# Broadcasting a score row to all partitions in two DMA loads of 512 columns instead of one of 1024 (a four-layer graph attention kernel)

## The chip, the cores and the metric

The kernel runs on one core of a Trainium2 chip. The metric is the device time of one execution in microseconds (us); lower is better. Engines are called PE (TensorE, matmuls), PEld (its weight loads), DVE (VectorE), ACT (ScalarE), POOL (GpSimd) and SP (SyncE, which here only issues DMAs).

## The reference: what is computed

16 graphs of 1024 nodes with 256 features, a 0/1 adjacency of 1024 x 1024 for each, and four attention layers in a row, each added to its input:

```python
h = jnp.maximum(_layernorm(x, axis=-1), 0.0)
x = x + _L0_gnn_ref(h, adj, ...)      # 4 heads of 64; the same for layers 1, 2; layer 3 has one head of 256
# inside a layer, for each head:
e = leaky_relu(s1[:, None] + s2[None, :], slope)     # s1, s2: one number a node, h @ (W a)
attention = softmax(where(adj == 0, -inf, e), axis=-1)
out = attention @ (h @ W)
```

Layer 2 adds a bias, a relu, the projected h and a layernorm over each head before its result is added.

## The kernel before

All the work is in `fast_path` (line 537). A *unit* is one layer of one graph. The 48 units with four heads (layers 0 to 2) run in the fixed order `ORDER` (lines 412 to 419), which mixes graphs so that one unit's preparation lies beside another's attention; the 16 units of layer 3 are fitted in between.

A unit is prepared in `prepare` (line 949): statistics, normalisation (`normal`), transposes and projection to `v` (`project`). For each head there is then one row of 1024 numbers, an exponential of the nodes' scores. The exponential of a sum under a leaky relu is a maximum of two products, so an attention tile needs only this row spread over all partitions, one number a partition (`fac`) and the mask.

The row gets to all partitions through DRAM. It is written to a scratch `line` (lines 1119 to 1121) and read back with an access pattern whose first dimension has step 0, so that each of 128 partitions receives the same 4 KB (lines 1123 to 1130):

```python
over = units.tile([P, N], F32, name="rows", bufs=ROWS)      # ROWS = 1; rows_one for layer 3
sp.dma_start(over, bass.AP(tensor=flat.tensor, offset=flat.offset + h * N, ap=[[0, P], [1, N]]))
```

There is one buffer `rows`, so the next head's load waits until ACT has copied the last row away. `spread_row` (line 1209) lets ACT copy the row to a two-bank PSUM tile `r`; `cover` (line 1218) lets DVE make eight tiles `p` of 128 x 1024 from it, each `max(r, fac) * mask`; `gather` (line 1278) lets PE multiply the tile's 64-column pieces with `v`, 65 columns at a time, into `po`; `evacuate` and `finish` take the sums away. For layer 3 `last_layer` (line 1396) reads `rows_one` in pieces.

The order of instructions on every engine is written by a planner at build time. `Plan` (line 443) holds for each engine when it would be free and adds an assumed cost for each instruction (`cost`, line 463; a DMA costs 400 ns of the SP queue). The loop at line 1589 takes, among all steps that could go next, the earliest one. A step is a piece of a Python generator up to its next `yield`, which names the engine of the next piece. Nothing is reordered later: each engine, SP's queue among them, runs its list in order and waits where a semaphore says so. The SP queue also carries the loads of `x_cur`, the transposing loads of the masks (`mask<-near`), weights, and the stores to `out`; the adjacency is cast on its way to the scratch `near` by DMAs of the POOL queue.

Of the kernel before, what the change touches and what calls it, by code (L numbers as in the profile page):

```python
# [20 lines left out]
P = 128  # L21
# [400 lines left out]
SPREAD = 0  # L422
SOONER = 300.0
AT_ONCE = -(10**6)
ACT_STATS = (0,)
SETTLE = 83.0
SECOND = 4000.0
# [109 lines left out]
def fast_path(  # L537
# [21 lines left out]
    nc = tc.nc  # L559
    ctx.enter_context(tc.manual_schedule())  # L560
    plan = Plan()
    pe, act, dve, pool, sp = (
        plan.engine(e, name)
        for e, name in (
            (nc.tensor, "PE"),
            (nc.scalar, "ACT"),
            (nc.vector, "DVE"),
            (nc.gpsimd, "POOL"),
            (nc.sync, "SP"),
        )  # L570
    )
    G, N, F = x.shape
# [82 lines left out]
    def bank():  # L655
        k = min(free_banks(), key=lambda k: banks[k])
        banks[k] = None
        if k >= BANKS:
            spare[0] += 1
            return ps_o.tile([P, 512], F32, name="po"), k  # L660
        return ps_p.tile([P, 512], F32, name=f"pp{k}"), k

    def drop(k: int):
        banks[k] = plan.now
# [17 lines left out]
    def wide_bank(dt=F32):  # L682
        k = wide_free.index(min(t for t in wide_free if t is not None))
        wide_free[k] = None
        return ps_r.tile([P, 4096 // mybir.dt.size(dt)], dt, name=f"r{k}"), k

    def leave_wide(k: int):
        wide_free[k] = plan.now
# [3 lines left out]
    def weights(layer: int):  # L692
# [43 lines left out]
        for k in range(KC):  # L736
            for c in range(KC):
                to = c * KC + k
                pe.transpose(pw[:, to * P : (to + 1) * P], given[:, k, c * P : (c + 1) * P], ident)
        yield "ACT", None, AT_ONCE  # L740
        if n == 1:
# [4 lines left out]
        drop(at)  # L746
        yield "PE", free_bank, AT_ONCE + 1
        pa, at = bank()
        for k in range(KC):
            for half in range(0, P, P // 2):  # L750
                for c in range(KC):
# [6 lines left out]
                    )  # L758
        yield "ACT", None, AT_ONCE
        act.copy(wa[layer][:, :, :, w : w + 2], pa[:, : KC * 2 * n].rearrange("p (k h c) -> p k h c", k=KC, h=n))  # L760
# [116 lines left out]
    def normal(es: list, rs: bass.AP):  # L877
# [25 lines left out]
        for e in es:  # L903
            yield "ACT", None, AT_ONCE
            e.hT = work.tile([P, KC, 2 * P], F32, name="hT", bufs=PAIRS)
# [5 lines left out]
    def project(e, i: int):  # L911
# [16 lines left out]
        e.read = plan.now  # L928
        yield "ACT", None, AT_ONCE
        act.copy(u.v[:, 2 * e.pair + i, :width], pv[:, :width])  # L930
# [18 lines left out]
    def prepare(u: "Unit"):  # L949
# [3 lines left out]
        width = n * (w + 2)  # L953
        by_act = layer in ACT_STATS and u.g.b >= BY_ACT and (layer < 3 or u.g.b < G - 2)
        yield "ACT" if by_act else "DVE", lambda: (
# [14 lines left out]
        if by_act:  # L970
            for i in range(2 * NB):
# [6 lines left out]
                b, c = i % NB, i // NB  # L978
# [48 lines left out]
        turned(pm, mine[:, 1, :])  # L1027
        yield "DVE", None, AT_ONCE
        top = small.tile([P, 1], F32, name="top", bufs=3)
# [16 lines left out]
        c = small.tile([P, 4, MAXN], F32, name="c", bufs=2)  # L1046
# [35 lines left out]
        if direct:  # L1082
# [20 lines left out]
            else:  # L1103
                yield "DVE", None, AT_ONCE
                over = units.tile([P, N], F32, name="rows_one", bufs=1)
# [16 lines left out]
        flat = line[: n * NB]  # L1122
        for h in range(len(u.row), n):
            yield "SP", lambda: (u.before is None or len(u.before.ps) == u.before.many * NB) if n == 1 else taken(ROWS, 4 * u.turn + h)
            if n > 1:
                over = units.tile([P, N], F32, name="rows", bufs=ROWS)
            else:
                over = units.tile([P, N], F32, name="rows_one", bufs=1)
            sp.dma_start(over, bass.AP(tensor=flat.tensor, offset=flat.offset + h * N, ap=[[0, P], [1, N]]))
            u.row.append((over, plan.now))  # L1130
        if n == 1:
            add(u.until + LATE, last_layer(u), plan.now)

    def turned(to, of):

        for half in range(0, P, P // 2):
            pe.matmul(to[half : half + P // 2, : P // 2], of, ident[:, half : half + P // 2])

    def taken(count: int, k: int):

        k -= count
        return k < 0 or main[k // H].weighed > k % H
# [59 lines left out]
    def row_due():  # L1202

        if rowed[0] == len(main) * H or rowed[0] * NB - at_tile[0] > ROW_LEAD or not free_wide():
            return False
        u, h = main[rowed[0] // H], rowed[0] % H
        return len(u.row) > h and max(u.row[h][1], free_wide())

    def spread_row():

        u, h = main[rowed[0] // H], rowed[0] % H
        rowed[0] += 1
        r, k = wide_bank()
        act.copy(r, u.row[h][0])
        u.across[h] = r, k, plan.now
        u.weighed += 1
# [179 lines left out]
    def last_layer(u: "Unit"):  # L1396

        due = lambda: (
            u.ready
            and hasattr(u, "flat")  # L1400
            and at_tile[0] >= u.gate
            and not row_due()
            and (late[0] < LATE_TILES or (at_tile[0] == len(tiles) and room() is not None and late[0] < TILES - 1))
        )
        free = lambda: due() and free_wide() and max(u.g.loaded, u.ready, free_wide())
        soon = lambda: u.ready and at_tile[0] == len(tiles) and room() and late[0] < TILES - 1 and max(u.ready, room())
        begun = at_tile[0]
        part = N // u.many
        for i in range(u.many):
            if i == 1:  # L1410
                add(u.until + LATE_SUMS, last_sums(u), plan.now)
            for j in range(0, NB, u.many):
                if u.kept:
                    yield "DVE", soon
                    late[0] += 1
                    cover_late(u, i, j, u.kept[0][:, i * part : (i + 1) * part])
                    continue
                yield "ACT", free, begun + LATE + int((i * NB + j) * SPREAD)
                late[0] += 1
                r, at = wide_bank()  # L1420
                act.copy(r[:, :part], u.row[0][0][:, i * part : (i + 1) * part])
                yield "DVE", room, at_tile[0]
                cover_late(u, i, j, r[:, :part])
                leave_wide(at)
        if u.kept:
            leave_wide(u.kept[1])
# [157 lines left out]
    def add(until, gen, ready, first=None):  # L1584
        jobs.append([until, ready, *(first or next(gen))[:2], gen])
# [3 lines left out]
    while True:  # L1589
        while begins and (begins[0][0] <= at_tile[0] or not jobs):  # L1590
            _, gen, until = begins.pop(0)
            add(until, gen, 0.0)
        can = []

        def offer(engine, ready, until, what):
            can.append((max(plan.free[engine], ready), until, engine, what))

        if row_due():
            offer("ACT", row_due(), at_tile[0], "row")
        if at_tile[0] < len(tiles) and room() is not None:  # L1600
            u, h, j = tiles[at_tile[0]]
            if h in u.across and u.g.loaded and u.ready:
                offer("DVE", max(u.across[h][-1], u.g.at[j % NQ2], u.ready, room()), at_tile[0] + SLACK, "cover")
        first = reach()
        if first:
            offer("PE", first[0], at_tile[0] + SLACK, "gather")
        for job in jobs:
            ready = job[3] is None or job[3]()
            if ready:
                ready = max(job[1], ready)  # L1610
                engine = job[2]
                offer(engine, ready, job[0], job)
        if not can:
            assert not jobs and not begins and at_tile[0] == len(tiles), "nothing can go on"
            break
        best = {}
        for e in ("SP", "POOL", "DVE", "ACT", "PE"):
            mine = [c for c in can if c[2] == e]
            if mine:
                first = min(c[0] for c in mine)  # L1620
                best[e] = min((c for c in mine if c[0] <= first + NEAR), key=lambda c: c[1])
        when, _, engine, what = min(best.values(), key=lambda c: c[0])
        plan.now, plan.last = when, None
        if what == "row":
            spread_row()
        elif what == "cover":
            cover(*tiles[at_tile[0]])
            at_tile[0] += 1
        elif what == "gather":
            gather()  # L1630
        else:
            step = next(what[4], None)
            if step is None:
                jobs.remove(what)
            else:
                wait = 0.0 if step[0] == engine else MARGIN.get(step[0], 40.0) if at_tile[0] < len(tiles) else 40.0
                what[0] = step[2] if len(step) > 2 else what[0]
                what[1:4] = [(when if step[0] == engine else plan.now) + wait, *step[:2]]


    nc.vector.tensor_scalar(bad[:, 2:3], greatest[:, G * LAYERS - 1 :], 1.0 / LEAST, bad[:, 3:4], ALU.is_le, ALU.is_lt)  # L1641
# [47 lines left out]
```

## Time and profile before

| | |
|---|---|
| time, median of 3 runs | 2668.85 us (2665.5 to 2671.96) |
| time of the profiled execution | 2667.53 us |
| its span, first to last instruction | 2665.8 us |
| granted TensorE clock, mean | 0.997 |
| loads of a row (`rows`, `rows_one`) | 190 + 13, 512 KB each |
| ACT copies of a row to PSUM | 190, 1021 ns each |
| DMA queue q1 (hardware) | 143088 packets, 159.10 MB |
| DMA queue q0 (POOL's, the `near` loads) | 67456 packets, 16.78 MB |
| HBM traffic | 191.77 MB read, 34.39 MB written |

Busy time is the union of an engine's instructions. In the waits view a row says who waited for whom, then the total in us, how often, and the longest. "issue" as the one waited for means that no semaphore explains the wait. In the timeline a row has the start, the length, the engine, the line, the operation, how many were merged (xN), and in brackets the idle time before it. Nearly all instructions carry line L515, the helper that records them, so they are told apart by tiles.

### The profile page before, as it was taken

Reading aid. Unit: us, or ns where it says so; the run is one execution under the profiler, and the core shown is the slowest. Engines: PE = TensorE matmul, PEld = TensorE weight load, DVE = VectorE, ACT = ScalarE, POOL = GpSimd, SP = SyncE. Lnnn points to the kernel's source line nnn. Section 1 sums busy time; section 2 is a strip of 40 time slices with the busy share of each in tenths; the row PEclk is TensorE's granted clock in tenths of the full one; section 3 lists DMA queues with packets and bytes.
Section 4 is the critical chain, followed back from the end, with each engine's and each line's share of the span. In section 5 each row is a group of like instructions: output and inputs, shape, how many; then the busy total and the mean of one; then the engine's idle time right before and its main releaser. Section 6 shows DMA issues by size and latency. Waiting matters only on the chain. (4 is left out here: it accounts for less than half of the span.)

```text
span 2665.8 us, 132436 instructions
## 1 busy us (share of the span) xinstructions
PE 2578.2 (97%) x59354; PEld 2207.9 (83%) x59354; DVE 2342.0 (88%) x3723; ACT 1272.3 (48%) x3378; POOL 1890.4 (71%) x3375
## 2 busy tenths in 40 slices
PE   9999999999999999999999999999999999899998
PEld 7888887787988788889888788988778798888775
DVE  6799998897999797889998897999888699998984
ACT  4633563654346456533564644356364553443441
POOL 5556888765778877747887875688787565977761
PEclk9999999999999999999999999999999999999999
DMA  8533233443132253313314441323334441111100
GB/s 133 84 75 73 59 69 69 76 87 71 64 66 63 63 85 82 76 57 77 72 55 82 88 72 59 83 50 75 74 74 79 83 85 57 53 47 55 40 23 32
DMA packets 211122, 184.44 MB, mean 69 GB/s; under 512 B 150640, under 2 KB 184560, under 8 KB 210544
## 3 DMA queue, kind: packets, MB, share of 16 engines
q1 hardware_dynamic: 143088, 159.10, 20.7%
q0 software_dynamic: 67456, 16.78, 10.3%
q8 instruction: 467, 7.65, 1.2%
q14 instruction: 111, 0.91, 0.1%
HBM read 191.77 MB, written 34.39 MB: 85 GB/s over the span
## 5 line engine op out<-in xcount | busy, mean ns | idle before, releaser
L515 DVE SCALAR_TENSOR_TENSOR p<-r,fac,mask 128x1024 f32<-128x1024 f32 (+2 forms) x2032 | 2075.7, 1079 | 159.8 <-PE pp L515 80.8
L515 PE MATMUL po<-v,p 128*64 128x65 f32 x32992 | 1060.9, 224 | 36.4 <-issue 15.8
L515 PEld LDWEIGHTS po<-v,p 128*64 128x64 f32 x32992 | 1021.5, 138 | 87.9 <-issue 30.8
L515 PEld LDWEIGHTS po<-v_flat,p 128*64 128x64 f32 x16384 | 507.8, 138 | 56.8 <-issue 24.4
L515 PE MATMUL po<-v_flat,p 128*64 128x65 f32 x16384 | 525.0, 223 | 29.4 <-issue 14.7
L515 PE MATMUL pp<-wa,hT 128*64 128x264 f32 (+1 forms) x4032 | 474.2, 385 | 0.1
L515 PE MATMUL pp<-v_one,p 128*64 128x257 f32 x3584 | 403.6, 380 | 3.2 <-ACT y L515 2.9
L515 PEld LDWEIGHTS pp<-wa,hT 128*64 128x64 f32 x4032 | 278.4, 137 | 132.1 <-ACT v L515 0.4
L515 PEld LDWEIGHTS pp<-v_one,p 128*64 128x64 f32 x3584 | 248.6, 136 | 128.0 <-ACT y L515 4.6
L515 POOL TENSOR_SCALAR hn<-x_cur,rs 128x256 f32<-128x256 f32 x504 | 274.6, 558 | 33.3 <-PE pp L515 29.3
L515 POOL TENSOR_TENSOR att<-att,inv 128x512 f32<-128x512 f32 x128 | 133.7, 1045 | 221.2 <-DVE inv L515 207.7
L515 ACT COPY att<-po 128x260 f32<-128x260 f32 x256 | 96.2, 376 | 377.1 <-PE po L515 353.1
L515 ACT COPY v<-pp 128x264 f32<-128x264 f32 (+1 forms) x392 | 148.5, 379 | 215.0 <-PE pp L515 213.8
L515 POOL TENSOR_TENSOR x_cur<-att,x_cur 128x512 f32<-128x512 f32 x190 | 225.8, 1188 | 14.9
L515 ACT COPY r<-rows 128x1024 f32<-128x1024 f32 x190 | 194.0, 1021 | 21.8 <-DVE p L515 15.5
L515 ACT ACTIVATE att<-att,s 128x64 f32<-128x64 f32 x512 | 190.9, 439 | 23.3 <-POOL s L515 23.0
L515 ACT ACTIVATE hT<-pp 128x512 f32<-128x512 f32 x250 | 136.4, 598 | 128.1 <-PE pp L515 127.4
L515 ACT ACTIVATE att<-po,inv 128x64 f32<-128x64 f32 x512 | 118.7, 321 | 145.6 <-DVE inv L515 143.6
L515 POOL TENSOR_TENSOR y<-y,x_cur 128x256 f32<-128x256 f32 x116 | 84.3, 732 | 131.6 <-ACT y L515 112.1
L515 POOL TENSOR_TENSOR v<-v,fac 128x512 f32<-128x512 f32 x131 | 136.2, 1064 | 11.5 <-ACT fac L515 11.4
L515 DVE BATCH_NORM_STATS2 st<-x_cur 128x6 f32<-128x256 f32 x400 | 138.3, 411 | 3.3 <-DMA x_cur<-in_x_dram 2.9
L515 PE MATMUL pp<-ident,hn 128*128 128x128 f32 x1000 | 137.0, 280 | 0.2 <-DVE row L515 0.2
(124 smaller groups left out, 2150.0 us busy)
## 6 DMA issues: line engine op xcount, KB each, us to landing
rows<-line SPq DMA_DIRECT2D x190, 512.0 KB
out_dram<-y SPq DMA_DIRECT2D x128, 128.0 KB
x_cur<-in_x_dram SPq DMA_DIRECT2D x112, 128.0 KB
near<-in_adj_dram POOLq DMA_DIRECT2D x112, 128.0 KB, 4.3
rows_one<-line SPq DMA_DIRECT2D x13, 512.0 KB
x_cur<-in_x_dram SPq DMA_DIRECT2D x4, 512.0 KB
line<-row SPq DMA_DIRECT2D x96, 8.0 KB
block<-in_adj_dram POOLq DMA_DIRECT2D x4, 256.0 KB, 10.4
```

Source lines behind the costliest of these rows:

```text
L515: r = call(*a, **k)
```

## The change

Each row is loaded by two DMAs of 512 columns (2 KB a partition) instead of one of 1024. The first is issued where the whole load was. The second is put on a list and issued behind the next step that the planner gives to SP; or when the planned time has gone 2.5 us further; or, at the latest, before ACT's copy that reads the row. The planner still books one load of 1024 columns. The diff, complete:

```diff
 AT_ONCE = -(10**6)
+PIECES = 2
+ROW_APART = 2500.0
 ACT_STATS = (0,)
...
                 over = units.tile([P, N], F32, name="rows_one", bufs=1)
-            sp.dma_start(over, bass.AP(tensor=flat.tensor, offset=flat.offset + h * N, ap=[[0, P], [1, N]]))
+            of = lambda c, size: bass.AP(
+                tensor=flat.tensor, offset=flat.offset + h * N + c, ap=[[0, P], [1, size]]
+            )
+            plan.spend("SP", *plan.cost("SP", "dma_start", (over, of(0, N)), {}), [flat.tensor.name])
+            size = N // PIECES
+            nc.sync.dma_start(over[:, :size], of(0, size))
+            for c in range(size, N, size):
+                pieces.append((plan.free["SP"], over[:, c : c + size], of(c, size)))
             u.row.append((over, plan.now))
...
+    pieces = []
+
+    def next_piece():
+
+        nc.sync.dma_start(*pieces.pop(0)[1:])
+
+    def all_pieces():
+
+        while pieces:
+            next_piece()
...
         r, k = wide_bank()
+        all_pieces()
         act.copy(r, u.row[h][0])
...
                 r, at = wide_bank()
+                all_pieces()
                 act.copy(r[:, :part], u.row[0][0][:, i * part : (i + 1) * part])
...
         plan.now, plan.last = when, None
+        while pieces and pieces[0][0] + ROW_APART < when:
+            next_piece()
+        waiting = len(pieces)
         if what == "row":
...
                 what[1:4] = [(when if step[0] == engine else plan.now) + wait, *step[:2]]
+        if engine == "SP" and waiting:
+            next_piece()
```

## The prediction

> **What bounds the kernel now.** First the page's busy times, then who waits for whom (all engines).
>
> ```profile
> PE 2578.2 (97%) x59354; PEld 2207.9 (83%) x59354; DVE 2342.0 (88%) x3723; ACT 1272.3 (48%) x3378; POOL 1890.4 (71%) x3375
> ```
> ```profile
> DVE p L515 <- PE pp L515: 80.8, 45, 4.9
> ...
> DVE p L515 <- PE po L515: 34.7, 30, 4.1
> DVE p L515 <- ACT r L515: 32.7, 8, 10.4
> ...
> PE po L515 <- issue: 30.5, 32, 2.6
> ...
> PE po L515 <- ACT att L515: 15.8, 16, 1.4
> ...
> PE po L515 <- DVE p L515: 9.4, 9, 2.7
> ```
>
> PE is the bound: it works 2578.2 of 2665.8 us, DVE waits for PE (80.8 + 34.7 us) far longer than PE for DVE (9.4 us). The largest item in PE's idle time is "issue", 30.5 us, a wait that no semaphore explains.
>
> What that wait is, the DMA queues tell. From the page, then from a window of 2.9 us and the 1.0 us after it:
>
> ```profile
> q1 hardware_dynamic: 143088, 159.10, 20.7%
> ...
> q8 instruction: 467, 7.65, 1.2%
> ```
> ```profile
> q1 hardware_dynamic: 132, 0.50, 51.5%
> ```
> ```profile
> q8 instruction: 1, 0.02, 5.5%
> q1 hardware_dynamic: 12, 0.02, 5.3%
> ```
>
> The timeline of PE and of SP around that window (2032.6 to 2036.5 us):
>
> ```profile
> 2027.65 9.15 PE L515 MATMUL po<-v,p 128*64 128x65 f32 x308
> 2037.83 3.95 PE L515 MATMUL po<-v,p 128*64 128x65 f32 x128 [1.02 <-issue]
> 2042.95 2.26 PE L515 MATMUL po<-v,p 128*64 128x65 f32 x71 [1.16 <-issue]
> ```
> ```profile
> 2032.64 5.29 SPq L515 DMA_DIRECT2D rows<-line  x2
> ```
>
> 467 packets of 16384 B, against 2 x 59354 PE instructions: one packet is 256 instructions, 128 matmuls with their weight loads. PE eats that in 3.95 us (the x128 row). So q8 brings PE its program, and "issue" is PE out of program. Here a row load is issued at 2032.64; q1 moves nearly all its 0.50 MB before q8's packet starts (at 2035.54, by the packet records); PE runs dry at 2036.81 and resumes 2.3 us after that start. The second row load (2037.93) does the same.
>
> It is not one case. I counted in the packet records when the 467 fetches start after the issue of the latest of the 203 row loads. By chance a half microsecond would hold about 18. There are 23 in the first half, then 9, 8, 4, 1 (0.5 to 2.5 us), then 19, 38, 27, 28, 24. Some 45 fetches are held back to behind the row. Sorting PE's stalls over 0.1 us by what moved in the 2.5 us before the late fetch: rows alone 17 stalls, 14.5 us; rows with `near` loads 4, 6.1 us; `near` alone 10, 8.4 us; the rest 8, 3.7 us.
>
> **The change part by part.** In the changed kernel the lists of PE, DVE, ACT and POOL are the same instruction for instruction; only SP's differs, by 203 more DMAs. And the words of the change mislead: 175 of the 203 second loads stand directly behind their first one, since the planner's next step is rarely SP's. 11 have an `x_cur` load between, 8 a store, 8 the other kind of row, 1 a mask transpose. So the halves are issued some 0.4 us apart.
>
> *SP's queue.* 203 issues of 0.327 us (the row loads' median) are 66 us more. SP spends 708 us waiting for ACT's copies alone, so they lie in idle time; an `x_cur` load or a store comes 0.4 us later. The list shows SP also waiting for the eighth DMA before to land; with two DMAs a row, eight reach less far back. Nearest rows: a row lands 3.8 us after issue, a store 1.9, `x_cur` 4.6. Bounds: 0, and 3 us where a burst meets it; I take 0.
>
> *Packets.* 25,984 packets of 4096 B (median 159 ns) become 51,968 of 2048 B, which the trace does not show. 1024 B packets take 46 ns, so a line gives 84: a row occupies a DMA engine 16 x 84 = 1344 ns, not 8 x 159 = 1272. Bounds: 16 x 46 = 736 and 16 x 159 = 2544 ns. I take 84, between two near rows: +0.07 us for a held fetch, 21 stalls x 0.07 = 1.5 us if nothing else changes.
>
> *The row lands later.* 0.4 us from the issue, some 0.1 from packets. ACT's copy starts 5.8 us (median) after its row has landed; 6 of 190 have under 0.4 us. ACT is idle half the time, and DVE's first tile of a row starts at least 2.2 us after the landing in all but one. That one is issued at 64.78 us: 1.73 us, and its second half goes behind a mask transpose that holds SP for 1.4 to 2.1 us. Cost between 0 and 1.5 us; I take 0.5. ACT's copy waits for two semaphores instead of one: between 0 and ACT's own idle time, taken as 0.
>
> *What a held fetch saves.* A load spends about 1.5 us on an engine (first packets 0.97 us after issue, most engines done at 2.46). If a fetch that arrives in the first half is let in between the halves, it waits up to 0.75 us less. Summing the smaller of stall and 0.75 us: 9.4 us over the 17 stalls by rows alone, and 2.9 over the 4 with `near`, of which I count half: 10.9 us. Does the engine switch there? The nearest rows are four pairs of `rows_one` and `rows` issued 0.5 to 0.8 us apart. In none did a fetch start within 3.6 us of the first issue; two started at 3.65 and 3.88, amid the second load, two at 4.86, when both were through. That speaks for a gap at the border of two DMAs (first load done at about 2.9, plus the 0.5 to 0.7 us that single rows show between their end and the fetch), not proof. Bounds: 0, and all 20.6 us of both groups. I take 10.9, since the long stalls, which make most of it, are those of fetches that came early.
>
> [...]
>
> **Sum.** 10.9 us less stall. PE also waits for ACT, DVE and POOL, some 40 us in all, so a part of what it gains is waited away: I take nine tenths, 9.8. Less 1 us for late rows and longer packets: 8.8. The profiled execution took 2667.53 us (its span 2665.8), 1.3 under the median of the runs; it would take 2658.7, the median about 2660.
>
> **Rivals.**
> - *The fetch still waits for both halves* (the change does not do what it says). For it: the halves stand back to back, and with two loads queued fetches at 4.86 us came last. Against: the two at 3.65 and 3.88. Then 0 to 3 us lost: 2669 to 2672.
> - *The split holds fetches longer.* Both halves go before the fetch and packets of 2048 B cost more than the line says. At 110 ns a row takes 16 x 110 = 1760, +0.49 us: 21 stalls x 0.49 = 10 us, and some 25 fetches now held without a stall begin to stall, at half of that, 6 us: about 2685. It decides from roughly 95 ns on. For it: in the pairs, packets of the first load took 290 to 440 ns once the second was queued. Against: 1024 B packets at 46 ns.
> - *The rows come too late.* If second halves landed 2 us later, 8 row changes where DVE already waits for ACT's copy (32.7 us) would not grow, as their rows landed over 2.4 us before; some 20 ACT copies would wait about 1 us: 5 to 10 us at most on ACT, half of it idle. 2669 to 2674. Against: only one second half lies behind a slow instruction.
>
> **Chances.** The fetch let in, 2650 to 2666: 0.58, of which 0.52 is faster by over 0.2% (5.3 us, about what a measurement of this kernel can tell from no change) and 0.06 within it. Fetch waits for both, or late rows at small price: 0.24, of it 0.04 faster by chance, 0.18 the same, 0.02 slower. Longer holds or late rows in earnest: 0.18, all slower. Together 0.56, 0.24, 0.18 + 0.02 = 0.20. The range leaves out the best of the first case (all 20.6 us gone) and the upper half of the last: 2649 to 2680. The likeliest case's own range is 2650 to 2666.
>
> **What would show it.** Right: PE's "issue" falls from 30.5 us to some 18 to 22; the stalls of about 1 us behind row loads go, those behind `near` stay; PE's busy time is unchanged; fetches start about 2.5 us after a row's first issue; 2048 B packets near 84 ns. Wrong: "issue" the same or higher, or a new row in which ACT's copy waits for `rows`. If "issue" falls and the time does not, PE's gain was waited away on DVE or ACT.

## The result, and the profile after

| | kernel before | kernel after |
|---|---|---|
| median of 20 runs each | 2667.16 us (2662.0 to 2671.96) | 2673.32 us (2665.38 to 2682.1) |
| ratio, 95% interval | 1 | 1.0024 [1.0016, 1.0032] |
| profiled execution, its span | 2667.53, 2665.8 us | 2665.38, 2663.5 us |

The change makes the kernel slower, by 0.24% or 6.2 us, where 0.3% faster was forecast. The profiled execution of after is the fastest of its 20 runs, 7.9 us under their median, so its totals must not be read as if they were the usual run's. That may be more than luck: of the kernels with a second DMA below, the change again was profiled in the second fastest of its 12 runs (7.4 us under their median), the adjacent halves in the fastest of 7 (9.9 us) and the small load in the fastest of 9 (5.3 us). Why is not known; their profiles show too little of the loss. What profiles show well is what does not vary: counts, sizes and order. First the page, busy times and queues:

```profile
PE 2581.0 (97%) x59354; PEld 2213.6 (83%) x59354; DVE 2342.1 (88%) x3723; ACT 1270.8 (48%) x3378; POOL 1885.4 (71%) x3375
...
q1 hardware_dynamic: 172320, 159.11, 21.6%
...
q8 instruction: 467, 7.65, 1.2%
```

The engines have the work they had (PE 2581.0 against 2578.2 us) and the program comes in the same 467 packets. q1 moves the same megabytes in 172320 packets instead of 143088, and its share of the DMA engines rises from 20.7 to 21.6%. Now who waits for whom, all engines:

```profile
DVE p L517 <- PE pp L517: 80.2, 45, 4.9
...
DVE p L517 <- PE po L517: 34.9, 30, 4.1
DVE p L517 <- ACT r L517: 33.0, 9, 10.4
...
PE po L517 <- issue: 27.4, 35, 2.3
...
PE po L517 <- ACT att L517: 14.8, 16, 1.4
...
PE po L517 <- DVE p L517: 12.3, 10, 2.7
...
ACT r L517 <- DMA rows<-line: 4.7, 2, 3.0
```

Each row stands where it stood before, within 3.1 us; the last one, ACT waiting for a row to land, was 3.1 us. "issue" fell from 30.5 to 27.4, not to the 18 to 22 of the forecast. Two more profiles of the same kernel, shown below, have 36.5 and 36.1 us (spans 2676.5 and 2675.4), and two more of the kernel before 35.2 and 31.5 us (2674.9 and 2670.4). One profile of each would have told the wrong sign.

The rows' DMA issues (duration of an issue, shortest/median/longest, and when the first and the last starts):

```profile
L1136 SPq DMA_DIRECT2D rows<-line x190: 319/322/396, 33.7 to 2539.5; - x190
L1147 SPq DMA_DIRECT2D rows<-line x190: 326/433/1962, 34.6 to 2539.9; - x190
```

The second halves follow 0.37 us (median) behind the first. The 51,968 packets of 2048 B take 84 ns (median), as estimated. The later half lands 4.4 us (median) after the first issue, where the whole row landed at 3.8.

What decides is when q8's packets start, counted from a row's first issue, in half microseconds from 0 to 5 us (the packet records, 467 fetches in each kernel; row loads some microsecond apart or less count as one):

```
before            23  9  8  4  1 19 36 29 26 26
before, second    20 13  8  3  1 15 37 33 25 29
before, third     19 19  4  1  1 13 49 19 29 33
after             18 16  3  3  5 20 20 32 32 23
after, second     25 11  6  3  3 14 19 40 30 25
after, third      27 12  7  4  4 16 21 33 33 23
```

In all three profiles of before the held fetches come out in a peak at 3.0 to 3.5 us (36, 37, 49); in all three of after that bin holds 19 to 21 and the peak is at 3.5 to 4.0 (32, 40, 33), in two of the three with as many in the next half microsecond.

The stretch in which the forecast wanted them, 2.0 to 3.0 us, has 25, 17 and 20 fetches against 20, 16 and 14. They are not the same kind of fetch. In the three profiles of after, 17, 16 and 17 fetches are followed, from the moment they end, by 8 or more packets of 2048 B, the last of which starts 0.9 to 1.15 us later. Eight packets are one DMA engine's share of a half (256 packets, 16 engines, two halves): these fetches were let in between the halves. One of them starts at 484.48 us, 2.98 us after the row's first issue, and takes 0.96 us; exactly 8 packets of the row start after it, from 485.43 to 486.45. The three profiles of before have no such fetch. The fetches that start 2.0 to 5.0 us after a row's first issue with 7 or fewer of its packets still to come fall from 134, 136 and 140 to 107, 104 and 103. So of the some 45 fetches that the row loads hold back, about a third is let in between the halves, and the others wait for both.

In PE's stalls over 0.1 us the two sides cancel near the row. Those of fetches that start 2.0 to 5.0 us after a row's first issue make 19.2, 24.3 and 24.8 us in the profiles of before and 17.4, 23.8 and 21.3 in those of after; all others make 12.1, 11.2 and 7.5 us before and 11.2, 13.9 and 16.0 after.

### The profile page after: what moved, and what is told of

Read it like the earlier page. It is cut to its first block, busy times and chain, and to the rows that moved or that the text cites. A ratio compares the mean times of both kernels' runs of the same rounds, so it can differ in the third digit from the quotient of the medians.

```text
span 2663.5 us, 132762 instructions
## 1 busy us (share of the span) xinstructions
PE 2581.0 (97%) x59354; PEld 2213.6 (83%) x59354; DVE 2342.1 (88%) x3723; ACT 1270.8 (48%) x3378; POOL 1885.4 (71%) x3375
## 3 DMA queue, kind: packets, MB, share of 16 engines
q1 hardware_dynamic: 172320, 159.11, 21.6%
## 5 line engine op out<-in xcount | busy, mean ns | idle before, releaser
L517 ACT COPY r<-rows 128x1024 f32<-128x1024 f32 x190 | 194.1, 1021 | 23.8 <-DVE p L517 14.7
```

Of the source, the lines that this page charges most:

```text
L517: r = call(*a, **k)
```

## The experiments

The expectations name three theories. The *program theory*: the time moves with PE's waits for its program, and fetches are let in between loads. The *window theory*: a row occupies the DMA engines for longer, from its first packet to its last, and so holds back more fetches. The *queue theory*: more DMAs make rows, stores and `x_cur` late. The one that the runs left was put in words only after the small load behind a whole row: **most of the some 45 fetches that the row loads hold wait for a second DMA directly behind a row's first as well, which moves the peak of their releases from 3.0 to 3.5 us to 3.5 to 4.0, and PE, which then waits longer for its program ("issue" 41.1 us with the small load against 31.5 before, on one chip), pays.** Rivals: the packets of 2048 B are what costs; the rows' second halves come too late; or a second DMA has a fixed price that has nothing to do with holding fetches. Each ratio is against runs of the kernel before on the same chip.

### The change again

The kernel after, unchanged.

> The changed kernel once more, for a second profile. The program theory (the time moves with PE's waits for its program, which the loads hold back; the first profile, 2665.4 us, was the fastest of 20 runs): time about 2673, and if this profile's execution is slower than the first by x us, PE's stalls (gaps with no semaphore behind them, 29.8 us in the first profile) are larger by about x. The queue theory (203 more DMAs make rows, stores and x_cur late): same time, but the additional us stand under waits of ACT for rows, DVE for r, or POOL and ACT for y, by 5 us or more in total, and PE's stalls stay near 30 us.

2685.67 us against 2676.28, 1.0035 [1.0019, 1.0052]. The loss is there on another chip, and its profile is one of the three above. Its span is 13.0 us longer than the first profile's, "issue" 9.1 us longer (36.5 against 27.4), and ACT's wait for rows no longer (4.4 us against 4.7): the time moves with PE's program, as the program theory had it, and not with late rows.

### How much the row loads hold PE back

```diff
+ONLY = 16
...
-            sp.dma_start(over, bass.AP(..., ap=[[0, P], [1, N]]))
...
+            nc.sync.dma_start(over[:, :ONLY], bass.AP(..., ap=[[0, P], [1, ONLY]]))
...
-        act.copy(r, u.row[h][0])
+        act.copy(r.rearrange("p (k c) -> p k c", c=ONLY), u.row[h][0][:, :ONLY].unsqueeze(1).to_broadcast([P, N // ONLY, ONLY]))
```

> Before, but each row load brings only 16 of the 1024 columns (64 B a partition) and ACT spreads these 16 over its 1024 columns: leaves out 63/64 of each row's load, so that the attention weights are others; every engine's list is the same. Program theory: the 14.5 us of stalls behind rows and most of the 6.1 us behind rows and near go, PE's stalls fall to 12 to 16 us, time 2645 to 2655. Queue theory and late rows: nothing waits for a row in before (3.1 us in all), so 2663 to 2668.

2646.38 us, 0.9891 [0.9871, 0.9911]. From its page and its waits:

```profile
q1 hardware_dynamic: 143088, 54.33, 9.5%
```
```profile
DVE p L516 <- PE pp L516: 79.4, 44, 4.9
...
PE po L516 <- issue: 12.1, 19, 1.3
```

The number of DMAs and packets is before's, their bytes are a third, DVE's wait for PE stays, and "issue" goes from 30.5 us to 12.1. Held fetches now start 2.0 to 3.0 us after a row's issue (54 of 467), and only two of the 20 stalls over 0.1 us that remain belong to such a fetch (0.73 and 1.24 us). So the premise of the forecast holds: row loads hold PE's program back, and what their bytes cost in all is about 30 us (2676.28 - 2646.38), more than the 20.6 us that the sorting of stalls gave as the most to be had.

### Packet size alone

One DMA a row, with its halves put 516 columns apart, so that it moves in 256 packets of 2048 B.

```diff
+WIDE = 516
...
-                over = units.tile([P, N], F32, name="rows", bufs=ROWS)
+                over = units.tile([P, 2, WIDE], F32, name="rows", bufs=ROWS)
...
+            of = bass.AP(tensor=flat.tensor, offset=flat.offset + h * N, ap=[[0, P], [N // 2, 2], [1, N // 2]])
+            sp.dma_start(over[:, :, : N // 2], of)
```

> Before, with one load a row as there, but the row in two halves 516 columns apart in SBUF, so that the one DMA has 256 packets of 2048 B. If the packets' size costs the time (twice as many packets beside near loads and fetches), about 2673 as in the changed kernel. If the number of DMAs costs it, 2667 plus or minus 1.5. The program theory has no firm view: a fetch still waits for the whole load, 1.34 instead of 1.27 us an engine, 2667 to 2669.

2677.88 us, 1.0002 [0.9989, 1.0015].

```profile
q1 hardware_dynamic: 169072, 159.10, 21.4%
```

The packets are there (143088 + 25984 = 169072), the loss is not: the second DMA costs, not the smaller packets. Its releases peak at 3.0 to 3.5 us (44 fetches), as before's do.

### The halves far apart

The second load begins one column earlier, so that it overlaps the first and has to wait until that has landed.

```diff
-                pieces.append((plan.free["SP"], over[:, c : c + size], of(c, size)))
+                pieces.append((plan.free["SP"], over[:, c - 1 : c + size], of(c - 1, size + 1)))
```

> The changed kernel, but the second load starts one column earlier and so waits for the landing of the first: the halves are about 3.3 us apart instead of 0.4. Program theory with fetches let in between: no fetch waits for more than one half (0.75 us), stalls behind rows fall from some 14 to under 5 us, time 2655 to 2662. Queue theory: SP's queue stands still for 2.9 us more at each row and rows land 3 us later, so ACT waits for rows in a quarter of the cases: 2680 or more.

2703.72 us, 1.0105 [1.0086, 1.0124]. SP's timeline and the waits:

```profile
1179.34 0.34 SPq L1136 DMA_DIRECT2D rows<-line  x1
1182.85 0.34 SPq L1147 DMA_DIRECT2D rows<-line  x1
```
```profile
ACT r L517 <- DMA rows<-line: 82.1, 30, 10.9
...
DVE p L517 <- ACT r L517: 48.7, 17, 10.6
...
PE po L517 <- issue: 24.9, 36, 1.7
```

With 3.3 us (median) between the halves, the fetches do come in between: stalls behind rows alone are 5.7 us in 9 (14.5 us in 17 before). But SP stands still for that long, a row lands 6.9 us (median) after its first issue, and ACT waits 82.1 us for rows where it waited 4 to 6 in the changed kernel. The program theory had under 5 us of such stalls and 2655 to 2662 us: it was near on the stalls and wrong on the time. What the gap gives is lost several times over in the rows.

### Always directly behind

```diff
-                pieces.append((plan.free["SP"], over[:, c : c + size], of(c, size)))
+                nc.sync.dma_start(over[:, c : c + size], of(c, size))
```

> The changed kernel, but every second load stands directly behind its first (28 of 203 no longer have another instruction between). Window theory (a row now occupies the DMA engines for longer, from its first packet to its last, and so holds back more fetches than the gap between the halves lets through): like the changed kernel, ratio to before 1.002 to 1.004. If the late second halves among the 28 cost the time (the rows at 44 to 74 us, behind mask transposes and loads of x_cur): 1.000 plus or minus 0.001.

2685.22 us against 2674.95, 1.0041 [1.0024, 1.0057].

```profile
PE po L517 <- issue: 36.7, 46, 2.3
...
ACT r L517 <- DMA rows<-line: 6.3, 5, 1.9
```

The place in the queue, which the words of the change are about, is not what costs: with no load or store between the halves the loss is as large. The rows are late by 6.3 us of ACT's waiting, on an engine that is busy 48% of the time, and DVE's wait for ACT's copy is 33.2 us as ever. The profile of before beside it (no change)

> The kernel before, unchanged, for a profile on the same chip as the next three. No theory expects a difference from its own runs; PE's stalls, the fetches held and the engines' time for a row are to be compared with the others' on this chip.

took 2676.77 us and gave the second row of the table above.

### A whole row and a small load behind it

The row comes in one load as before. Behind it, 8 columns are loaded into a tile that nobody reads.

```diff
+            more = units.tile([P, 8], F32, name="more", bufs=1)
+            nc.sync.dma_start(more, bass.AP(tensor=flat.tensor, offset=flat.offset + h * N, ap=[[0, P], [1, 8]]))
```

> Before, with its one load of 1024 columns, and directly behind each a second load of 8 columns (32 B a partition) into a tile of its own that nobody reads: 203 more DMAs on SP's queue and its semaphores, no split. Queue theory: like the changed kernel, ratio to before 1.002 to 1.004. Window theory: 1.000 to 1.001, since these packets are short and do not stretch the row.

2684.65 us, 1.0035 [1.0024, 1.0045]: the same loss, with 4 KB more and no row split.

```profile
PE po L515 <- issue: 40.8, 51, 2.3
...
DVE p L515 <- ACT r L515: 32.9, 8, 10.4
```

The rows are in time (DVE waits 32.9 us for their copies, 32.7 before), and "issue" is higher than in any profile of before. Its releases: 3 at 2.5 to 3.0 us, 15 at 3.0 to 3.5 and 55 at 3.5 to 4.0, where before has 13 to 19, 36 to 49 and 19 to 33. This is the sharpest single run: the row, its packets and its landing (3.9 us) are before's, one tiny DMA stands behind it, and the peak moves. The window theory, with 1.000 to 1.001, missed it: the second DMA needs only 4 KB to cost. Here too some 10 fetches are let in between the row and the small load (8 packets of 32 B start after each), which does not make up for the others: the stalls of fetches 2.0 to 5.0 us after a row's issue are 29.0 us, against 19.2 to 24.8 before.

### Four loads

`PIECES = 4`.

> The changed kernel with four loads of 256 columns a row. Window theory: each further load stretches a row by up to 0.4 us, so three times the change's cost, ratio to before 1.006 to 1.012, with more fetches held and half of them with short stalls. Theory that fetches slip in between pieces (my prediction's): faster than the changed kernel, 0.996 to 0.999.

2693.77 us, 1.0069 [1.0051, 1.0088], with "issue" at 46.6 us and ACT's waiting for rows at 26.1. Three DMAs more a row cost about twice what one costs, and some of that is late rows. The releases move on: most start at 4.5 to 5.0 us (31).

### A small load later

The small load reads the row's own buffer, so it goes out when the row has landed, some 3.9 us after it.

```diff
+            more = units.tile([P, 8], F32, name="more", bufs=1)
+            nc.sync.dma_start(more, over[:, :8])
```

> Before, and behind each row load a second one of 8 columns that reads the row's buffer and so is issued only when the row has landed, some 3.9 us after its issue (e7's stood 0.4 us behind). ACT's copy does not wait for it. Queue-joining theory (a load issued before the held fetch has its turn goes ahead of it and prolongs the hold): nothing joins, ratio to before 1.000 to 1.0015, stalls behind rows as in before. Theory of a fixed price for each DMA wherever it stands: 1.003 to 1.004, as e7. SP's queue stands still for 3.9 us at each row, which can delay stores and x_cur; e4 had that too, so a part of a rise can be that, to be seen in POOL's and ACT's waits for y.

2688.34 us against 2674.59, 1.0045 [1.0028, 1.0061]. The peak of releases is back at 3.0 to 3.5 us (46 fetches), as in before, where nothing stands behind the row either. The time is no lower, and above the 1.000 to 1.0015 of the theory, though "issue" is 34.8 us, among before's. SP stands still for each landing, some 3.9 us, and waits appear or grow (ACT's for the stores of `y` was 8.0 us before):

```profile
ACT y L515 <- DMA out_dram<-y: 36.9, 15, 4.6
...
ACT seen L515 <- DMA mask<-near: 9.6, 3, 7.5
...
DVE p L515 <- DMA mask<-near: 7.2, 2, 6.5
```

So this run confirms the release and settles nothing about the time.

### Half the bytes

Rows, line and buffer in bf16, which rounds the rows; one load of 2 KB a partition. Then the same with two loads of 512 columns.

```diff
-        line = dram.tile([MAXN * NB, P], F32, name="line")
+        line = dram.tile([MAXN * NB, P], BF16, name="line")
...
-                over = units.tile([P, N], F32, name="rows", bufs=ROWS)
+                over = units.tile([P, N], BF16, name="rows", bufs=ROWS)
```

> Before, with the row, its scratch line and its broadcast buffer in bf16 (one load of 2 KB a partition; rounds each row's exponentials to 8 bits; ACT widens them when it copies): half the bytes, the same number of DMAs, every engine's list the same. The tiny row gave 0.989 with 1/64 of the bytes. If the hold is a fixed part and one that goes with the bytes: about half of that, 0.993 to 0.996. If only the number of DMAs counts: 1.000.

> e10 with each row in two loads of 512 columns, directly one behind the other. Price of the second load by e6 and e7: 0.3 to 0.4 per cent above e10. By my prediction's theory (fetches let in between): below e10.

One load: 2657.49 us, 0.9933 [0.9917, 0.9948]. Two: 2655.47, 0.9931 [0.9916, 0.9946]. The waits of the first, then of the second:

```profile
PE po L515 <- issue: 18.4, 21, 1.9
```
```profile
PE po L515 <- issue: 19.1, 28, 2.3
```

Shorter loads are what the split was meant to give, and with half the bytes they do give it. With two loads there are more stalls (28 for 21), but their sum and the time are not different. A fixed price of 0.35% for the second load would have given 0.9968; that is outside the interval. The releases move here too, from a peak at 3.0 to 3.5 us (34 fetches) to one at 3.5 to 4.0 (34). So the price is not the same wherever a release moves; that PE has more program in hand when the loads before were short is a likely reason, and not shown.

### Two tiny loads

The tiny row with a second load of 16 columns behind it.

```diff
...
+            for c in (0, ONLY):
+                nc.sync.dma_start(over[:, c : c + ONLY], bass.AP(..., ap=[[0, P], [1, ONLY]]))
```

> e2 (a row load of 16 columns, the rest left out) with a second load of 16 columns directly behind, so 32 of 1024 columns are brought and 31/32 are left out. If a second load costs because it prolongs the hold by its own 0.4 us, also where there are hardly any bytes: 0.3 to 0.4 per cent above e2's 0.9891. If it costs only behind a long load: e2's 0.9891 plus or minus 0.0015.

2654.56 us, 0.9918 [0.9903, 0.9932], where one tiny load had 0.9891: +0.27%, with intervals that overlap. "issue" goes from 12.1 to 14.2 us. By the reading of the two bf16 kernels a second load behind so short a first should cost next to nothing. The releases say how it can cost something: they peak at 3.0 to 4.0 us (32 and 30 in the two bins) instead of 2.0 to 3.0, the row lands 3.9 us after its first issue instead of 2.5, and seven stalls, 2.8 us in all, now belong to fetches that start at 3.2 to 3.4 us. So here a second DMA prolongs the hold by about 1 us with hardly any bytes. Whether its price is the same everywhere stays open: this run speaks for it, the two bf16 kernels speak against.

### Fewer and longer loads

Two heads by one DMA, in bf16: as many bytes at a time as a row of before, in 95 loads instead of 190.

```diff
+        many = 1 if n == 1 else 2
...
+                over = units.tile([P, many, N], BF16, name="rows", bufs=ROWS)
...
+            nc.sync.dma_start(over, bass.AP(..., ap=[[0, P], [N, many], [1, N]]))
```

> e10 with two heads' rows in one load (4 KB a partition again, 95 loads of rows instead of 190; same bytes as e10, rounding as there; every engine's list the same). If a load's price is a fixed part (e7, e12: 0.3 per cent for 203) and one that goes with the bytes: 0.14 per cent below e10, 0.9915 to 0.9925. If a hold costs only where it is longer than PE's margin, long holds cost more than in proportion: 108 loads of which each holds like one of the 203 of before, whose bytes cost 1.1 per cent: 0.994 to 0.996.

2658.18 us, 0.9937 [0.9919, 0.9956], the time of one head a load. "issue" is 25.1 us in 32. The row lands 3.7 us after its issue, 3.3 with one head a load. Half the DMAs gain nothing here; that each holds a fetch longer is an estimate from these landings. The ratio lies between the two ranges expected and its interval reaches into both, so it decides nothing between a price a DMA and one for the length of a hold.

### Three more profiles

Before, after, and the small load behind a whole row, once more, for their packet records.

> The kernel before, a third profile, for the counts of held fetches: releases (fetch starts) after a row's issue peak at 3.0 to 3.5 us, nearly none at 2.0 to 2.5; PE's stalls 30 to 40 us.

> The changed kernel, a further profile on the same chip as the third of before. Window theory: 15 to 20 fetches start at 2.0 to 2.5 us after a row's first issue (before: 1 or 2), the others as late or later than in before, and PE's stalls are 3 to 10 us above those of the third profile of before. My prediction's theory: 10 us below.

> e7 again (one full load and an 8-column load directly behind), for its counts on the same chip: the peak of releases 0.5 us later than before's, at 3.5 to 4.0 us, none at 2.0 to 2.5; PE's stalls 5 to 10 us above before's.

2672.28, 2677.22 and 2683.42 us; "issue" before `po` 31.5 us in 34, 36.1 in 48 and 41.1 in 48. The peaks of release: 3.0 to 3.5 us (49 fetches), 3.5 to 4.0 (33), 3.5 to 4.0 (56, with 17 in the bin before). One expectation was mistaken: the 15 to 20 fetches that were to start 2.0 to 2.5 us after the first issue had been counted from the later of the two loads. From the first, there are 4.

How a fetch that waits for both halves looks in the kernel after: PE's timeline, SP's, and the DMA queues from 1178.0 to 1181.6 us and from 1181.6 to 1182.8 (packets, MB, share of 16 engines).

```profile
1174.78 7.43 PE L517 MATMUL po<-v,p 128*64 128x65 f32 x240
1183.94 3.25 PE L517 MATMUL po<-v,p 128*64 128x65 f32 x105 [1.73 <-issue]
```
```profile
1177.97 0.34 SPq L1136 DMA_DIRECT2D rows<-line  x1
1178.35 0.44 SPq L1147 DMA_DIRECT2D rows<-line  x1
```
```profile
q1 hardware_dynamic: 283, 0.52, 54.6%
```
```profile
q8 instruction: 1, 0.02, 5.1%
q1 hardware_dynamic: 5, 0.00, 1.0%
```

The halves are issued 0.38 us apart. All 0.52 MB of both move with no packet of q8 among them; the fetch starts at 1181.74 (packet records), 3.77 us after the first issue, and PE, dry since 1182.21, resumes 2.2 us after that start. The small load behind a whole row gives the same picture:

```profile
1795.82 6.42 PE L515 MATMUL po<-v,p 128*64 128x65 f32 x207
1803.68 3.12 PE L515 MATMUL po<-v,p 128*64 128x65 f32 x81 [1.44 <-issue]
```
```profile
1797.36 0.32 SPq L515 DMA_DIRECT2D rows<-line  x1
1797.72 0.43 SPq L1131 DMA_DIRECT2D more<-line  x1
```

The fetch starts at 1801.19, 3.83 us after the row's issue.

## Why the prediction was wrong, point by point

- **PE is the bound, and "issue" is PE waiting for its program:** right. Over the 16 profiles of this study without the two in which SP stands still (halves far apart, late small load), the span follows 2630.2 us + 1.22 x PE's "issue" (before all its tiles), with a correlation of 0.98 and a scatter of 2.5 us. The kernel with one DMA of smaller packets lies farthest off, 7.5 us above.
- **Rows hold fetches back:** right, and undersized (30 us by the tiny row).
- **Halves 0.4 us apart:** right, 0.37. **Packets:** right, 84 ns. A line between two near rows was good.
- **"What a held fetch saves" is the step that failed.** Its condition was that a fetch arrives in the first half; its sum of 10.9 us then took every stall behind a row as if its fetch did, and charged the fetches that are not let in 0.07 us. A gap at the border of two DMAs is real: 16 or 17 fetches a profile use it. But some 45 are held, and the others wait for both halves: the first rival, for two fetches of three. Their releases move from 3.0 to 3.5 us to 3.5 to 4.5. In the profiles the stalls near a row stay as they were (17.4 to 23.8 us against 19.2 to 24.8) where half of 20.6 was to go, and all other stalls are 11.2 to 16.0 us against 7.5 to 12.1. The four pairs in the trace of before had shown just this mixture: the fetches at 3.65 and 3.88 us leave 10 and 8 of the pair's 256 packets behind them, so they stood between the loads, as the prediction read them; the two at 4.86 did not. Two cases of four do not carry a step that holds the whole sum.
- **The rival's price was too low as well.** It said 0 to 3 us, from 0.07 us for each of 21 held fetches, and SP's queue cost was taken as 0. The change (twice), the adjacent halves and the small load measure 6 to 10 us (1.0024, 1.0035, 1.0041, 1.0035). The cost is not that of longer packets (84 ns; 1.0002 with one DMA), nor mainly of late rows (1.0035 with the rows in time): a second DMA moves the release of most held fetches by about 0.5 us, also where it has 4 KB only, where 0.07 was counted. 21 stalls x 0.5 would be about 10 us, an estimate. For the small load it fits (its stalls near a row are 29.0 and 30.4 us, some 7 above before's). For the split it is not shown: near a row it has what the gap saves on the other side, and its profiles, of executions 7 to 10 us faster than the median where that can be told, do not say where the median run loses its 6 to 9 us.
- **Longer holds** (second rival) had the right effect for the wrong reason: it was to come from packets above 95 ns, and they take 84. **Late rows** are small with two loads and show with four.
- **Smaller slips, without effect:** the sum takes off 1 us for late rows and longer packets, where the parts before it had 0.5 and 1.5. 2037.93 us is where the issue of the second row load in the example ends; it starts at 2037.59.

A half is 8 packets an engine (256 packets over 16 engines). In the runs about a third of the held fetches enter behind them (16 or 17 a profile); the others wait for both halves, and most wait for a tiny load behind a whole row (55 and 56 start at 3.5 to 4.0 us, where before has 19 to 33). What decides which of them enters, no run shows.

Open: why a second load costs nothing in bf16 and perhaps 0.27% behind a tiny row, so whether a part of the price is fixed; what lets one fetch in at the border of two DMAs and not the next; and where in a usual run the split loses its time. Halves spaced by some microseconds with the rows loaded that much earlier, which might give the gap without the late rows, were not tried.

## What to carry to other kernels

Where the bound engine shows "issue" gaps, hold them against the packets of the instruction queue: here some 45 of 467 started right behind the kernel's own row loads, and those loads' length was on the path (0.9891 with 1/64 of their bytes), and their number too (1.0035 with a small load behind each), though q1's share of the DMA engines was 20.7%. Cutting the load in two back to back made a gap that a third of the held fetches found, and added a DMA to the hold of the others (1.0024); halving its bytes did help (0.9933 with rows in bf16, the quickest version found that still loads whole rows, with or without the cut). And where runs spread over 0.6%, as after's 20 do, read the sign from the timed ratio and the mechanism from counts that repeat, not from one profile's span. A histogram of starts alone can mislead too: before and after have nearly as many fetches at 2.0 to 3.0 us, but only what each leaves behind it tells which stood between two loads.

## What was not expected of the hardware

A load of 8 columns, 4 KB in all, delayed most of the instruction fetches held behind a 512 KB load by half a microsecond: 36 to 49 of them start at 3.0 to 3.5 us without it, 15 and 17 with it; at 3.5 to 4.0 us it is 19 to 33 without it, 55 and 56 with it.

Three of PE's stalls in the kernel before were also followed by 3.41 us (clock records of the trace) at half the granted clock. Two of them lie in these five stretches of 3.4 us, the first and fourth with a wait for DVE of 2.55 and 2.74 us (busy time and count of PE, PEld, DVE, ACT, POOL, then the granted clock, the DMA engines' share and GB/s):

```profile
2313.70:2317.10 3.40, 1.26 (x35) 1.16 (x37) 3.40 (x6) 0.57 (x2) 3.02 (x9) 1.00 0.02 5
2317.10:2320.50 3.40, 3.40 (x67) 3.40 (x68) 3.40 (x5) 3.40 (x10) 3.12 (x4) 0.50 0.01 2
2320.50:2323.90 3.40, 3.40 (x122) 3.40 (x120) 3.40 (x3) 0.39 (x2) 3.40 (x6) 1.00 0.48 154
2330.80:2334.20 3.40, 1.31 (x36) 1.17 (x38) 3.40 (x6) 0.00 (x0) 3.09 (x9) 1.00 0.05 14
2334.20:2337.60 3.40, 3.40 (x68) 3.40 (x68) 3.40 (x4) 0.00 (x0) 3.02 (x7) 0.50 0.00 0
```

After 3.4 us in which PE worked 1.26 or 1.31 us, the clock is 0.50 for the next 3.4 us and PE gets through 67 or 68 matmuls instead of 122: 54 x 27.9 ns (3.40 us over 122) = 1.5 us lost on top of the stall. The third, at 484.2 us, comes after an "issue" gap of 2.25 us, with PE at work for 1.15 of the 3.40 us ahead of it. The half clock could be a reason for a slope above 1 in the relation of span and "issue", but that is not shown: the profiles of before have 3, 5 and 6 stretches of half clock ahead of the last microseconds, those of after 4, 4 and 2. In the three of the first profile PE was busy for 34 to 39% of the 3.4 us ahead; what makes the clock fall, these traces do not show.
